# 64-wide matmul products in column pairs, one merged weight in the first message round, and a GpSimd memset behind each gather, in a four-layer graph kernel

## The chip, the cores and the metric

The kernel runs on one NeuronCore of one Trainium2 chip. The metric is device time in microseconds (us). Three runs of the kernel before gave 3177.02, 3179.41 and 3182.76 us; the median is 3179.41 us. A profile comes from one further execution, recorded by the hardware profiler.

Engines are named as the profile names them: PE (TensorE matmul), PEld (its weight loads), DVE (VectorE), ACT (ScalarE), POOL (GpSimd), SP (SyncE, which issues DMAs).

## The reference

There are B = 16 graphs of N = 1024 nodes with C = 64 channels, a dense weighted adjacency of 1024 x 1024 for each (about 1.6% of it non-zero), H = 128 hidden channels, and four layers, each of which adds its result to `x` and normalises over channels:

```
x = layernorm(x + (adj @ (x @ W0) + b0))                 # layer 0
adj_d = dilate(adj)            # drops some neighbours by rank
agg = sum over tau of w * quantile_tau(x of the kept neighbours)
x = layernorm(x + (relu((x + agg) @ W1 + b1) @ W2 + b2)) # layer 1
h = x @ W_embed                                           # layer 2
for l in range(3): h = relu(adj @ (h @ Wl[l] + bl[l]))
x = layernorm(x + h @ W_proj + b_proj)
t = adj @ x                                               # layer 3
x = layernorm(x + where(t > 0.5, 1, 0))
```

The quantiles of layer 1 need, for every node and channel, the neighbours' values in order. That is where most of the VectorE work lies.

## The kernel before

Nodes lie in T = 8 tiles of P = 128. Everything is float32 unless it is named otherwise. The work on one graph is cut into generator functions whose `yield` values are estimated times:

- `words_of` (L502) loads eight rows of the adjacency (`arow`, by SP), transposes each on PE (L439), copies it out on ACT (L441), packs its non-zero pattern into words (L526, L536), and runs layer 0 through `Layer0.feed` (L464) and `Layer0.end` (L472 to L490). The transposed rows go to DRAM (`adjd`, L532).
- `front` and `listing` turn the words into a sorted list of neighbour numbers per node (`idx`), sort the nodes by degree, and write the table of `x` rows to DRAM (`table`).
- `gathered` (L808) fetches neighbour rows. Slot k of a tile of 128 nodes is one indirect DMA of 128 rows x 66 floats from the table, issued by GpSimd at L815. The eight tiles form five groups (`GROUPS`, L30). Partly filled slots are packed, so that one graph takes 122 gathers of whole slots and 7 of packed ones. A group's gathers land in a buffer of tag `x`, of which there are four. So the gathers of a group wait until the buffer of the fourth group before it has been summed.
- `masked` (L847) marks the slots that don't count (ACT L868) and makes the quantile weights. `quantiles` (L891) sorts each group's slots by a comparison network on DVE (L906). `summed` (L916) scales the wanted ranks (ACT L932) and adds them on PE (L936).
- `back` (L1122) is the rest of layer 1, and layers 2 and 3. `to_nodes` (L955) brings the aggregate back from degree order to node order by one-hot products in bf16 (L979) and adds x (L985). Two products, `residual` and `layernorm` follow. Then `to_channels` (L362) and the product with `we_sb` (L1185) make the embedding, and each of three message rounds multiplies by `wl_sb` (L1196), copies (L1199), and multiplies by the adjacency (L1207), followed by a relu (L1210). Layer 3 is `aggregate` (L372, product L377), a transpose back (L1219), a comparison and a layernorm.

The order in which the instructions stand on each engine is fixed at build time: a heap at L1266 takes the generator with the smallest due time, lets it record its next step, and puts it back with its yield value added (times a stretch factor). The due times come from `LENGTHS` (L52), whose sum is 192.06 us for a graph, and from constants such as `BACK` and `WORDS`. While graph b sorts its groups, the gathers run one to two groups ahead, `words_of` and `front` run for the next graph, and `back` for the graph before.

Some products have only 64 output channels, so that the stationary operand has 64 columns: L464, L377, L979 and L985. They use columns 0 to 63 of the array, and their results lie in PSUM partitions 0 to 63. The two halves of the 1024 nodes are then made one after the other, each with a PSUM bank and an ACT copy of 64 x 512 of its own. In `Layer0` the upper half of the `ax` tile receives x transposed, so that one product with `w0_sb` (W0 above an identity) makes both the new value and the residual; to transpose two tiles at once, `xt` has an extra tile of zeros in front.

Of the kernel before, what the change touches and what calls it, by code (L numbers as in the profile page):

```python
# [10 lines left out]
F32 = mybir.dt.float32  # L11
# [9 lines left out]
P = 128  # L21
# [132 lines left out]
def kernel(  # L154
# [102 lines left out]
    top = const.tile([P, T, K], F32, name="top")  # L257
    nc.vector.memset(top, 0.0)
    flags = const.tile([1, B + 1], I32, name="flags")
    qw = const.tile([P, Q], F32, name="qw")  # L260
    ntau = const.tile([P, Q], F32, name="ntau")
    for s, (tau, w) in enumerate(zip(TAUS, QWEIGHTS)):
# [11 lines left out]
    def load(name, shape, src):  # L274
        t = const.tile(shape, F32, name=name)
        nc.scalar.dma_start(t, src)
        return t


    w0_sb = const.tile([2 * C, C], F32, name="w0_sb")  # L280
    nc.scalar.dma_start(w0_sb[:C, :], w0)
    nc.vector.tensor_copy(w0_sb[C:, :], ident[C:, C:])
    w1_sb = load("w1_sb", [C, H], w1)
    b1_sb = load("b1_sb", [H, 1], b1.unsqueeze(1))
    w2_sb = load("w2_sb", [H, C], w2)
    we_sb = load("we_sb", [C, H], we)
    wl_sb = load("wl_sb", [H, NL, H], wl.rearrange("l i o -> i l o"))
    wp_sb = load("wp_sb", [H, C], wp)

# [5 lines left out]
        nc.vector.tensor_scalar(m, m, 1.0 / C, None, op0=ALU.mult)  # L295
        nc.vector.tensor_scalar(v, v, m, None, op0=ALU.subtract)

    for v, n in ((w0_sb, 2 * C), (w2_sb, H), (wp_sb, H)):
        centred(v, n)


# [17 lines left out]
    ones16 = const.tile([S, P], BF16, name="ones16")  # L319
    nc.vector.memset(ones16, 1.0)  # L320

    def add_bias(bank, first, n, times):

        nc.tensor.matmul(bank[:, :times * n], ones16,
                         bias16[:, first:first + n].unsqueeze(1).to_broadcast([S, times, n]),
                         start=True, stop=False)
# [1 line left out]

    mask_u8 = const.tile([B * T, P], U8, name="mask_u8")
    nc.scalar.dma_start(mask_u8, nodemask.rearrange("b (t p) -> (b t) p", p=P))  # L330
    mask_f = const.tile([B * T, P], F32, name="mask_f")
    nc.vector.tensor_copy(mask_f, mask_u8)
    mask = const.tile([P, B * T], F32, name="mask")
    pm = ps.tile([P, HALF], F32, tag="mm", name="pm", bufs=2)
# [7 lines left out]
    def psum_mm():  # L342
        return psum("mm", 2)

    def psum_tp():
        return psum("tp", 2)
# [12 lines left out]

    def to_channels(dst, src):  # L362

        for h in range(NH):
            pt = psum_mm()
            for i in range(TH):
                nc.tensor.transpose(pt[:C, i * P:(i + 1) * P], src[:, h * TH + i, :], ident)
            yield 1.5
            nc.scalar.copy(dst[:, h * HALF:(h + 1) * HALF], pt[:C, :])
            yield 1.0  # L370

    def aggregate(dst, adjT, src, bank):  # L372

        for h in range(NH):
            pa = bank()
            for m in range(T):
                nc.tensor.matmul(pa[:C, :], src[:, m, :], adjT[:, h * TH:(h + 1) * TH, m, :],  # L377
                                 start=(m == 0), stop=(m == T - 1))
                yield 1.3
            nc.scalar.copy(dst[:, h * HALF:(h + 1) * HALF], pa[:C, :])  # L380
            yield 0.7

    def layernorm(u, y, who, mean=False):

# [33 lines left out]
        return a  # L418

    def load_x(b):  # L420
        xt = act.tile([P, T + 1, C], F32, tag="x", name="xt")
        nc.vector.memset(xt[:, 0, :], 0.0)
        nc.sync.dma_start(xt[:, 1:, :], one(x, b).rearrange("o (t p) c -> p (o t) c", p=P))
        return xt

    def transposed(b, block, then):
# [25 lines left out]
    class Layer0:  # L452
# [6 lines left out]
        def feed(self, t, at):  # L459
            if t % TH == 0:  # L460
                self.bank = psum_ax()
            cols = slice((t % TH) * P, (t % TH + 1) * P)
            for m in range(T):
                nc.tensor.matmul(self.bank[:C, cols], self.xt[:, m + 1, :], at[:, m, :],  # L464
                                 start=(m == 0), stop=(m == T - 1))
            yield 2.4
            if t % TH == TH - 1:
                h = t // TH
                nc.scalar.copy(self.ax[:C, h * HALF:(h + 1) * HALF], self.bank[:C, :])
                yield 0.7  # L470

        def end(self, y):  # L472
            for h in range(NH):
                pt = psum_tp()
                for i in range(TH):

                    two = self.xt[:, h * TH + i:h * TH + i + 2, :].rearrange("p t c -> p (t c)")
                    nc.tensor.transpose(pt[:, i * P:(i + 1) * P], two, ident)
                yield 1.0
                nc.scalar.copy(self.ax[C:, h * HALF:(h + 1) * HALF], pt[C:, :])  # L480
                yield 0.7
            pz = psum_ax()
            add_bias(pz, 0, C, T)
            for t in range(T):
                nc.tensor.matmul(pz[:, t * C:(t + 1) * C], self.ax[:, t * P:(t + 1) * P], w0_sb,
                                 start=False, stop=(t == T - 1))
                if t % 2:
                    yield 0.7
            yield 1.0
            yield from layernorm(nodes(pz), y, "0")  # L490
# [317 lines left out]
    def gathered(st, g):  # L808
# [5 lines left out]
        def gather(dst, index):  # L814
            nc.gpsimd.indirect_dma_start(  # L815
                out=dst, out_offset=None, in_=st["table"],
                in_offset=bass.IndirectOffsetOnAxis(ap=index, axis=0))

        whole = [(i, t, k) for i, t in enumerate(tiles) for k in range(n)
                 if k < len(ROWS[t]) and ROWS[t][k] == P]  # L820
# [134 lines left out]
    def to_nodes(dst, st):  # L955


        ag = st["ag"]
        pieces = act.tile([P, S, T, C], BF16, tag="msg", name="pieces")
        for i in range(S):  # L960
            nc.scalar.copy(pieces[:, i], ag)
            yield 0.8
            if i + 1 < S:
                nc.vector.tensor_tensor(ag, ag, pieces[:, i], ALU.subtract)
                yield 0.8
        st["moved"] = True
        banks = [psum_mm() for _ in range(NH)]
        for s in range(T):
            ones_at = tmp.tile([P, N], BF16, tag="ones_at", name="ones_at", bufs=2)
            if st["b"] == B - 1 and s % 3:  # L970
                nc.vector.tensor_scalar(ones_at, iota, st["minus"][:, s:s + 1], 0.0,
                                        op0=ALU.add, op1=ALU.is_equal)
            else:
                nc.scalar.activation(ones_at, iota, AF.Abs, bias=st["minus"][:, s:s + 1])  # L974
                nc.scalar.activation(ones_at, ones_at, AF.Relu, bias=1.0, scale=-1.0)  # L975
            yield 1.9
            for h, bank in enumerate(banks):
                for i in range(S):
                    nc.tensor.matmul(bank[:C, :], pieces[:, i, s, :],  # L979
                                     ones_at[:, h * HALF:(h + 1) * HALF],  # L980
                                     start=(s == 0 and i == 0), stop=False)
            yield 1.7
        for h, bank in enumerate(banks):
            for i in range(TH):
                nc.tensor.matmul(bank[:C, i * P:(i + 1) * P], st["x1"][:, h * TH + i, :], ident,  # L985
                                 start=False, stop=(i == TH - 1))
            yield 1.2
            nc.scalar.copy(dst[:, h * HALF:(h + 1) * HALF], bank[:C, :])
        yield 1.0


# [28 lines left out]
    def general(b):  # L1020
# [44 lines left out]
        xc = act.tile([P, T, R], F32, tag="xc", name="xc", bufs=LIVES)  # L1065
        st["x1"] = xc[:, :, :C]
        run(l0.end(st["x1"]))
        xT = act.tile([C, N], F32, tag="chan", name="x1T")
        run(to_channels(xT, st["x1"]))
        xrow = dram.tile([C, N], F32, tag="xrow", name="xrow", bufs=1)  # L1070
        nc.sync.dma_start(xrow, xT)
        st["agg"] = act.tile([P, T, C], F32, tag="x3", name="agg")
        with tc.For_i(0, T, 1) as t:
            nb = tmp.tile([P, N], F16, tag="nb", name="nb")
# [47 lines left out]
    def back(st):  # L1122
# [31 lines left out]
            return act.tile([P, T, C], F32, tag=tag, name=name)  # L1154

        def chan(name):
            return act.tile([C, N], F32, tag="chan", name=name)


        oT = chan("oT")  # L1160
# [8 lines left out]
        for h in range(NH):  # L1169
            cols = slice(h * HALF, (h + 1) * HALF)  # L1170
            ph = psum_mm()
            nc.tensor.matmul(ph, w1_sb, oT[:, cols], start=True, stop=True)
            yield 1.3
            nc.scalar.activation(hT[:, cols], ph, AF.Relu, bias=b1_sb)
            yield 0.7
        x2 = node_tile("x2", "x2")
        yield from residual(hT, w2_sb, C, x1, x2)

        x2T = chan("x2T")
        yield from to_channels(x2T, x2)  # L1180
        hT = act.tile([H, N], F32, tag="hT", name="h0T")
        for h in range(NH):
            cols = slice(h * HALF, (h + 1) * HALF)
            ph = psum_mm()
            nc.tensor.matmul(ph, we_sb, x2T[:, cols], start=True, stop=True)  # L1185
            yield 1.3
            nc.scalar.copy(hT[:, cols], ph)
            yield 0.7
        for l in range(NL):
            msg = act.tile([P, T, H], F32, tag="msg", name="msg")  # L1190
            for h in range(NH):
                pg = psum_mm()
# [20 lines left out]
        yield from residual(hT, wp_sb, 2 * C, x2, x3)  # L1213

        tT = chan("tT")
        yield from aggregate(tT, adjT, x3, psum_mm)
        pt = psum_mm()
        for t in range(T):
            nc.tensor.transpose(pt[:, t * C:(t + 1) * C], tT[:, t * P:(t + 1) * P], ident[:C, :C])  # L1219
        yield 2.0  # L1220
        u = wide_u("u3")
        nc.vector.scalar_tensor_tensor(u, nodes(pt), 0.5, x3, op0=ALU.is_gt, op1=ALU.add)
# [93 lines left out]
```

## Time and profile before

| what | value |
|---|---|
| median of three timed runs | 3179.41 us |
| span of the profiled execution | 4328.2 us |
| PE busy, PE weight loads busy | 2647.8 us, 1635.7 us |
| DVE busy | 2822.0 us |
| ACT busy | 1914.0 us |
| POOL busy | 2160.8 us |
| instructions recorded | 46055 |
| mean granted TensorE clock | 0.764 of full speed |
| DMA | 282.54 MB, mean 65 GB/s |

The profiled execution is known by its span alone: 4328.2 us from the first to the last instruction of the core, 1148.8 us more than the median of the timed runs. "Busy" is the time in which an engine had an instruction under way. Matmul ends are modelled, and spans on POOL are rough, so the distance from one start to the next is the better measure on these two. A matmul of two float32 operands leaves two records; a transpose or a bf16 product leaves one.

### The profile page before, as it was taken

How to read it: one execution, taken by the hardware profiler on the slowest of the kernel's cores; microseconds unless marked ns; L12 is line 12 of the kernel's file. 1: busy time of each engine (PE TensorE's matmuls, PEld its weight loads, DVE VectorE, ACT ScalarE, POOL GpSimd, SP SyncE). 2: the span in 40 equal slices, each digit the busy share in tenths (PEclk: the TensorE clock that was granted, in tenths of full speed). 3: DMA queues.
4: the chain of work that ended last, by engine and by line, in shares of the span. 5: the costliest groups of instructions: out<-in, count | busy, mean ns of one | idle time of the engine just before them, and what ended most of it. 6: DMA issues, size and time to landing. Idle time of an engine off the chain costs nothing.

```text
span 4328.2 us, 46055 instructions
## 1 busy us (share of the span) xinstructions
PE 2647.8 (61%) x13765; PEld 1635.7 (38%) x13766; DVE 2822.0 (65%) x6935; ACT 1914.0 (44%) x6153; POOL 2160.8 (50%) x2078
## 2 busy tenths in 40 slices
PE   6034285675848567584755758476575848456478
PEld 5023152443525244352533435253343525233243
DVE  6058383865849486594857668485766859476671
ACT  2034352634536264453535455363545536253641
POOL 1715626455454645546465464546545554645600
PEclk8566597787969778796877879687787969768688
DMA  3212121322222132222213222231322222111210
GB/s 107 42 50 70 34 67 37 104 54 78 73 71 84 40 101 56 78 77 74 77 39 90 64 83 76 65 84 40 100 60 79 78 80 71 39 57 24 62 43 3
DMA packets 169056, 282.54 MB, mean 65 GB/s; under 512 B 99485, under 2 KB 102112, under 8 KB 166880
## 3 DMA queue, kind: packets, MB, share of 16 engines
q1 hardware_dynamic: 67584, 142.01, 9.9%
q0 software_dynamic: 66048, 69.88, 9.1%
q10 hardware_dynamic: 35168, 67.62, 4.1%
q8 instruction: 114, 1.87, 0.2%
q14 instruction: 142, 1.16, 0.1%
HBM read 204.33 MB, written 71.44 MB: 64 GB/s over the span
## 4 chain that ended last, share of the span: by engine, by line
another core or an unknown queue 28%; DVE 25%; PE 23%; ACT 16%; issue 7%; DMA 0%; ACTq 0%; DVEq 0%
DVE g L906 7%; PE mm L1207 7%; DVE s L906 7%; ACT g L868 6%; ACT ones_at L974 3%; PE ax L464 3%; ACT ones_at L975 2%; PE tp L439 2%; PE mm L377 2%; PE pa L936 2%; PE mm L1196 2%; ACT g L932 1%; PE mm L1141 1%; DVE top L707 1%
## 5 line engine op out<-in xcount | busy, mean ns | idle before, releaser
L815 POOL DMA_INDIRECT g<-table,idx x1952 | 2045.4, 1048 | 1919.7 <-PE pa L936 666.8
L1207 PE MATMUL mm<-adjB,msg 128*128 128x512 f32 x1536 | 769.6, 621 | 109.1 <-issue 82.4
L936 PE MATMUL pa<-g,ident 128*128 128x128 f32 (+1 forms) x1600 | 376.0, 360 | 430.1 <-ACT g L932 300.5
L868 ACT ACTIVATE g<-g,bias 128x64 f32<-128x64 f32 (+9 forms) x2272 | 596.8, 341 | 47.9 <-DVE bias L864 29.2
L906 DVE TENSOR_TENSOR s<-g 128x256 f32<-128x256 f32 (+9 forms) x944 | 531.3, 588 | 64.5 <-ACT g L868 55.5
L936 PEld LDWEIGHTS pa<-g,ident 128*128 128x128 f32 x1600 | 312.3, 248 | 574.0 <-ACT g L932 347.1
L906 DVE TENSOR_TENSOR g<-s 128x256 f32<-128x256 f32 (+8 forms) x864 | 473.4, 573 | 9.0 <-DVE s L906 3.0
L932 ACT ACTIVATE g<-g,w 128x64 f32<-128x64 f32 x1552 | 397.8, 341 | 17.2 <-DVE w L912 13.6
L1207 PEld LDWEIGHTS mm<-adjB,msg 128*128 128x128 f32 x1536 | 268.7, 197 | 301.1 <-issue 270.7
L1147 DVE TENSOR_TENSOR u<-mm,mb 128x512 f32<-128x512 f32 x32 | 22.1, 691 | 463.1 <-remote 313.5
L464 PE MATMUL ax<-at,xt 128*64 128x128 f32 x1920 | 284.5, 310 | 17.4 <-issue 17.4
L377 PE MATMUL mm<-adjB,x 128*64 128x512 f32 x512 | 272.6, 666 | 36.3 <-issue 31.3
L979 PE MATMUL mm<-ones_at,pieces 128*64 128x512 bf16 x768 | 213.0, 420 | 119.0 <-ACT ones_at L975 77.1
L464 PEld LDWEIGHTS ax<-at,xt 128*64 128x64 f32 x1920 | 250.2, 158 | 81.2 <-issue 79.1
L439 PE MATMUL tp<-ident,arow 128*128 128x128 f32 x1024 | 181.7, 309 | 156.2 <-remote 66.4
L399 DVE TENSOR_REDUCE ln_v<-sq 128x8 f32<-128x512 f32 x64 | 43.6, 681 | 296.4 <-issue 156.8
L439 PEld LDWEIGHTS tp<-ident,arow 128*128 128x128 f32 x1024 | 140.9, 162 | 205.1 <-issue 131.7
L441 ACT COPY at<-tp 128x512 f32<-128x512 f32 x240 | 139.0, 580 | 177.2 <-remote 122.3
L906 DVE TENSOR_TENSOR g<-g,s 128x256 f32<-128x256 f32 (+5 forms) x432 | 199.1, 464 | 15.1 <-remote 5.0
L906 DVE TENSOR_TENSOR g<-g 128x256 f32<-128x256 f32 (+8 forms) x304 | 200.7, 660 | 11.2 <-remote 4.0
L1219 PE MATMUL mm<-ident,tT 64*128 64x64 f32 x128 | 25.7, 295 | 293.9 <-ACT tT L380 207.4
L1210 ACT ACTIVATE hlT<-mm 128x512 f32<-128x512 f32 x96 | 57.4, 598 | 296.4 <-PE mm L1207 123.7
(225 smaller groups left out, 4361.9 us busy)
## 6 DMA issues: line engine op xcount, KB each, us to landing
arow<-in_adj_dram SPq DMA_DIRECT2D x128, 512.0 KB
adjd<-at ACTq DMA_DIRECT2D x120, 512.0 KB
adjB<-adjd SPq DMA_DIRECT2D x15, 4096.0 KB
g<-table,idx POOLq DMA_INDIRECT x1952
table<-xc ACTq DMA_DIRECT2D x16, 264.0 KB
xt<-in_x_dram SPq DMA_DIRECT2D x16, 256.0 KB
out_dram<-y SPq DMA_DIRECT2D x16, 256.0 KB
stage<-table,packed POOLq DMA_INDIRECT x112
```

Of the source, the lines that this page charges most:

```text
L377: nc.tensor.matmul(pa[:C, :], src[:, m, :], adjT[:, h * TH:(h + 1) * TH, m, :], start=(m == 0), stop=(m == T - 1))
L439: nc.tensor.transpose(pt[:, i * P:(i + 1) * P], a[:, j * P:(j + 1) * P], ident)
L441: nc.scalar.copy(at[:, h * TH:(h + 1) * TH, :], pt.rearrange("p (i n) -> p i n", n=P))
L464: nc.tensor.matmul(self.bank[:C, cols], self.xt[:, m + 1, :], at[:, m, :], start=(m == 0), stop=(m == T - 1))
L815: nc.gpsimd.indirect_dma_start(out=dst, out_offset=None, in_=st["table"], in_offset=bass.IndirectOffsetOnAxis(ap=index, axis=0))
L868: nc.scalar.activation(v, v, AF.Identity, bias=bias[:m, i, k:k + 1])
L906: nc.vector.tensor_tensor(box(bufs[mode >> 1 & 1], d, run, sd, count), box(bufs[mode >> 3], a, run, sa, count), box(bufs[mode >> 2 & 1], b ...
L932: nc.scalar.activation(slots(g, bufs[0], lo + r, lo + r + 1)[:, i, 0, :C], slots(g, bufs[at[r]], lo + r, lo + r + 1)[:, i, 0, :C], AF.Iden ...
L936: nc.tensor.matmul(pa[:, :(e - k) * nt * C], ident, rows_.rearrange("p (k c) -> p k c", c=R)[:, :, :C], start=(j == 0), stop=(j == len(run ...
L974: nc.scalar.activation(ones_at, iota, AF.Abs, bias=st["minus"][:, s:s + 1])
L979: nc.tensor.matmul(bank[:C, :], pieces[:, i, s, :], ones_at[:, h * HALF:(h + 1) * HALF], start=(s == 0 and i == 0), stop=False)
L1207: nc.tensor.matmul(pg, msg[:, m, :], adjT[:, h * TH:(h + 1) * TH, m, :], start=(m == 0), stop=(m == T - 1))
```

## The change

- **Column pairs.** The products with 64 stationary columns are issued in twos. One of a pair writes PSUM partitions 0 to 63, the other 64 to 127 of the same bank, on columns 0 to 63 and 64 to 127 of the array. In `to_channels`, `aggregate` and `to_nodes` the two are the two halves of the nodes; in `Layer0.feed` they are the even and the odd tiles of the sum, which the next product adds up, since `w0_sb` now holds W0 twice. A channel tile is 128 x 512 instead of 64 x 1024, and one ACT copy takes the place of two. `Layer0.end` adds x by a second product with `self_sb`. Transposes of 64 columns in `to_channels` become products with the identity.
- **Merged weight.** `wel_sb` = W_embed Wl[0] with the bias folded in is made once at the start. The first message round becomes `aggregate` of x + 1 (64 channels), one product with `wel_sb`, and the relu. The embedding product, the first product with `wl_sb` and the first 128-wide product with the adjacency are gone.
- **Memset.** `gather` issues a GpSimd memset of a tile `pause` of 128 x 256 bytes after every indirect DMA.

The constants of the planner are the same; the yield values of the changed steps are smaller or fewer. In the built program PE has 14711 instructions of work instead of 15044 (both with the fallback branch, which was not run), and POOL has one memset after each of its gathers.

```diff
+    pause = const.tile([P, 2 * P], U8, name="pause")
...
+    self_sb = const.tile([2 * C, 2, C], F32, name="self_sb")
+    nc.vector.memset(self_sb, 0.0)
+    w1_sb = const.tile([2 * C, H], F32, name="w1_sb")
+    for h in range(2):
+        half = slice(h * C, (h + 1) * C)
+        nc.scalar.dma_start(w0_sb[half, :], w0)
+        nc.vector.tensor_copy(self_sb[half, h, :], ident[half, half])
+        nc.scalar.dma_start(w1_sb[half, :], w1)
...
+    wel_sb = const.tile([2 * C, H], F32, name="wel_sb")
+    pe = ps.tile([P, HALF], F32, tag="mm", name="pe", bufs=2)
+    for h in range(2):
+        half = slice(h * C, (h + 1) * C)
+        nc.tensor.matmul(pe[half, :H], share16[:, half], bias16[:, 3 * C:3 * C + H],
+                         start=True, stop=False)
+        nc.tensor.matmul(pe[half, :H], weT, wl_sb[:, 0, :], start=False, stop=True)
+    nc.vector.tensor_copy(wel_sb, pe[:, :H])
...
+    def rows_of(t, h):
+        return t[h * C:(h + 1) * C]
...
-    def aggregate(dst, adjT, src, bank):
-        for h in range(NH):
-            pa = bank()
-            for m in range(T):
-                nc.tensor.matmul(pa[:C, :], src[:, m, :], adjT[:, h * TH:(h + 1) * TH, m, :],
+    def aggregate(dst, adjT, src, bank, tiles):
+        pa = bank()
+        for m in range(T):
+            for h in range(NH):
+                nc.tensor.matmul(rows_of(pa, h), src[:, m, :], adjT[:, tiles[h], m, :],
                                  start=(m == 0), stop=(m == T - 1))
-                yield 1.3
-            nc.scalar.copy(dst[:, h * HALF:(h + 1) * HALF], pa[:C, :])
-            yield 0.7
+            yield 1.3
+        nc.scalar.copy(dst, pa)
+        yield 0.7
...
             for m in range(T):
-                nc.tensor.matmul(self.bank[:C, cols], self.xt[:, m + 1, :], at[:, m, :],
-                                 start=(m == 0), stop=(m == T - 1))
-            yield 2.4
+                nc.tensor.matmul(rows_of(self.bank, m % 2)[:, cols], self.xt[:, m, :], at[:, m, :],
+                                 start=(m < 2), stop=(m >= T - 2))
+            yield 1.6
...
+                nc.tensor.matmul(pzt, self.ax[:, t * P:(t + 1) * P], w0_sb, start=False, stop=False)
+                nc.tensor.matmul(pzt, xT[:, t // 2 * P:(t // 2 + 1) * P], self_sb[:, t % 2],
                                  start=False, stop=(t == T - 1))
...
                 in_offset=bass.IndirectOffsetOnAxis(ap=index, axis=0))
+            nc.gpsimd.memset(pause, 0)
...
-            for h, bank in enumerate(banks):
-                for i in range(S):
-                    nc.tensor.matmul(bank[:C, :], pieces[:, i, s, :],
+            for i in range(S):
+                for h in range(NH):
+                    nc.tensor.matmul(rows_of(bank, h), pieces[:, i, s, :],
...
-        x2T = chan("x2T")
-        yield from to_channels(x2T, x2)
+        x2p = act.tile([P, T, C], F32, tag="msg", name="x2p")
+        nc.scalar.activation(x2p, x2, AF.Identity, bias=ones)
+        yield 1.0
+        gT = chan("gT")
+        yield from aggregate(gT, adjT, x2p, psum_mm,
+                             [slice(h * TH, (h + 1) * TH) for h in range(NH)])
...
-                nc.tensor.matmul(ph, we_sb, x2T[:, cols], start=True, stop=True)
+                nc.tensor.matmul(ph, rows_of(wel_sb, h), rows_of(gT, h), start=True, stop=True)
...
-        for l in range(NL):
+        for l in range(1, NL):
```

## Prediction

> **What bounds the kernel now.** I read the profile in the order page, GpSimd's waits, stages, chain of waits. The page first:
>
> ```profile
> span 4328.2 us, 46055 instructions
> PE 2647.8 (61%) x13765; PEld 1635.7 (38%) x13766; DVE 2822.0 (65%) x6935; ACT 1914.0 (44%) x6153; POOL 2160.8 (50%) x2078
> another core or an unknown queue 28%; DVE 25%; PE 23%; ACT 16%; issue 7%; DMA 0%; ACTq 0%; DVEq 0%
> L815 POOL DMA_INDIRECT g<-table,idx x1952 | 2045.4, 1048 | 1919.7 <-PE pa L936 666.8
> L1207 PE MATMUL mm<-adjB,msg 128*128 128x512 f32 x1536 | 769.6, 621 | 109.1 <-issue 82.4
> ```
>
> The span is 1149 us above the median of 3179 us. The chain names the excess: 28% of 4328 is 1212 us of waits for nothing that the program contains. In these stretches PE, ACT and DVE stand still together while POOL goes on gathering. 4328 - 1212 = 3116, near the median, so I take these waits as belonging to the profiled execution and subtract 1149 us from its sums. That is an assumption; no view proves it. The shares of the page then mislead: POOL's 50% is of the wrong span. Its own rows tell more:
>
> ```profile
> 96.05 1.13 POOL L815 DMA_INDIRECT g<-table,idx  x1 [92.94 <-DVE nb L526]
> 97.48 0.95 POOL L815 DMA_INDIRECT g<-table,idx  x1 [0.30 <-issue]
> ...
> 4114.67 1.45 POOL L815 DMA_INDIRECT g<-table,idx  x1 [0.30 <-issue]
> ```
>
> The columns are start, duration, engine. A gather takes 0.95 us when nothing disturbs it, and 0.30 us lie before the next even though it waits for nothing: one per 1.25 us. The waits of POOL give that gap in total:
>
> ```profile
> POOL g L815 <- PE pa L936: 666.8, 42, 80.5
> POOL g L815 <- issue: 566.6, 1858, 0.5
> ```
>
> "issue" is this gap, 1858 times (0.305 us each). The stages before, during and after the gathers:
>
> ```profile
> 0.00:96.00 96.00, 58.83 (x551) 50.72 (x553) 65.84 (x244) 23.23 (x59) 2.45 (x14) 0.84 0.31 94
> 96.00:4115.60 4019.60, 2417.51 (x12660) 1498.03 (x12658) 2672.22 (x6485) 1821.06 (x5889) 2157.84 (x2064) 0.76 0.24 67
> 4115.60:4328.20 212.60, 171.41 (x557) 87.00 (x557) 83.94 (x208) 69.70 (x205) 0.52 (x1) 0.85 0.06 23
> ```
>
> The numbers are the window, its length, and busy PE, PEld, DVE, ACT, POOL. The middle stage, less the excess, is 4019.6 - 1149 = 2871 us for 16 graphs. In it POOL needs 2157.8 busy + 566.6 + 34.7 (gaps before whole and packed gathers) = 2759 us, or 96%; DVE 2672, 93%; PE 2418, 84%. So the tightest engine is the one that the page shows as half idle. POOL has 2871 - 2759 = 112 us left over the whole run, 0.054 us for each of its 2064 gathers.
>
> **Part 1, the memset.** It adds 2064 instructions to POOL, in order behind each gather. Each waits for the memset before it (the same tile), which ended a gather earlier, so the wait is free; but the next gather is queued behind the memset, and `masked` (ACT and DVE) waits for the gathers of its group. No such memset stands in the trace; the nearest are those of the start:
>
> ```profile
> L215 POOL MEMSET tri<- 128x128 f16 x1 | 0.2, 195 | 0.0
> masks.py:197 POOL MEMSET ident<- 128x128 f32 x1 | 0.2, 205 | 0.3 <-POOLq L1302 0.3
> L1302 POOL MEMSET const-float32-0.0<- 128x1 f32 x1 | 0.1, 99 | 0.1
> ```
>
> From 1 to 128 elements the duration rises by 106 ns, 0.83 ns an element; two-byte elements take as long as four-byte ones, so I count elements and not bytes. 256 elements: 0.21 us, and about 0.03 us to start it (the one-element memsets start 0.02 to 0.03 us apart). **Bounds**: below zero I exclude, since no row shows a gather made shorter by an instruction before it; zero, if the memset fits into the 0.30 us gap; 0.085 us, if four bytes are written at once (64 x 0.83 + 30 ns); 0.24 us if it is added whole. Which? The same 0.3 us also stands between the end of PE's last `pa` product and a gather that waited for it (2491.70 to 2491.97), with POOL idle before. So it looks like starting work of the gather itself, after its release, and not like a hole. The Trainium skill, "GPSIMD Engine Reference", Instruction dispatch, speaks both ways: each of the eight cores goes on to the next instruction when its own share is done, and a pair of cores makes the descriptors. By that rule the other six would have the memset for nothing, but the pair, which sets the pace of gathers, pays it whole. By the rule 256 elements at its 1.03 cycles and 1.2 GHz are 0.22 us plus dispatch; by the row 0.24. I take 0.24 us, nearest to the measured memsets: 2064 x 0.24 = **+495 us** on POOL.
>
> **Part 2, the pairs.** A matmul of two float32 operands is two records. One graph has, with spacings from stretches in which they ran close together:
>
> - L464: 128 records; 16 of them filled 1.96 us, with their 16 weight loads 1.72 us. So 15.7 us.
> - L377: 32 records, 16.6 us.
> - L979: 48 records of bf16, 12 in 2.75 us: 11 us.
> - L985: 16 records, as L464: 2 us.
>
> If the two of a pair run together, half goes: 23 us. Here the Trainium skill has a rule against it: "TensorE: Matmul & The Clock Gate", The mechanism, says that a weight load overlaps a running matmul only if the two use different row groups, and column pairs share their rows. The trace shows loads beside matmuls of one tile now, at 1.72 of 1.96 us. By the row L464 can't fall below its loads: 13.8 us instead of 7.9; by the rule, loads and matmuls in turn, a pair would take 4 x 0.107 + 0.246 = 0.67 us, more than today's 0.49, and L464 21.7 us. For 512 columns loads are small (0.15 of 0.52 us), and half is nearly reached. I take -2, -8, -5 and 0: 15 us for a graph. Two products more with `self_sb` (16 records of 0.12 us) cost 2.
>
> **Part 3, the merged weight.** Gone: 32 records of L1207 (13.7 us by the chain of the last graph), 16 of L1196 on `h0T` (2.4), two bias products (0.8), the 8 transposes at L367 (1.2); in their place an aggregate in pairs, 8.3 us. PE saves 10 us. ACT saves about six copies of 0.58 us and pays two: 2 us. Parts 2 and 3 together: -23 us of PE for each graph.
>
> **What it is worth.** PE is at 84%, and behind it stand POOL and DVE, of which these parts save nothing. Only where PE sets the end does all of it count. That is the tail, 212.6 us with 171 of PE:
>
> ```profile
> 4278.10 13.73 PE mm L1207 x32
> 4298.87 16.57 PE mm L377 x32
> ```
>
> There the last graph's `back` loses 8 (L377), 10 (the round), and a few us at L979, and the graph before it some of the same: -30 us. The start (two waves of L464, 7.1 us each) gives 2 to 7; I say 5. The order on POOL and SP is unmoved; SP issues the same transfers. PE and ACT record `back` and `words_of` in fewer, shorter steps, so these stand earlier among the sort's steps: what DVE waits for comes no later.
>
> **Sum.** Start 96 - 5, gathers 2759 + 495, tail 213 - 30: 91 + 3254 + 183 = **3528 us**, with POOL never waiting. I predict 3530. DVE's cover is gone then: each group's `masked` waits for its gathers, and the freed PE time is idle. The likeliest case reaches from 3430 (0.19 us a memset) to 3570 (some waits remain).
>
> **Rivals.**
>
> 1. *The memset is hidden in the 0.30 us gap.* For it: the memset is shorter than the gap. Against it: the gap behaves as start-up of the gather. POOL's floor is then 91 + 2759 + 183 = 3033 us, and DVE's lies close (93%). From 3179 go 35 us at the two ends and about half of POOL's 112 us of waits, since `summed` frees buffers earlier: 3090 us. Range 3040 to 3140.
> 2. *The memset costs 0.085 us.* 2064 x 0.085 = 175; 3033 + 175 = 3208, and the waits that stay make it up to 3280.
> 3. *The excess isn't the profiler's alone.* If gathers at full pace also hold the other engines up in timed runs, a slower pace loosens that. For it: the stretches in which PE, ACT and DVE stand still end a few us after POOL stops (POOL stops at 2479.2, DVE goes on at 2484.2). Against it: the timed runs have no room for more than 3179 - 3116 = 63 us of it. With those gone too, 3020.
> 4. *The pairs don't overlap.* Worth at most the 35 us at the ends: 3560 instead of 3528, inside the first case.
>
> Rival 1 turns into the forecast at one point: where the memset adds more than (112 + 35) / 2064 = 0.07 us to a gather.
>
> **How the numbers follow.** Forecast 0.55; rival 1 0.31; rival 2 0.08 (nearly all of it slower); rival 3 0.06. Rival 4 is within the forecast. A difference of 0.2% (6 us) is about what a measurement of this kernel can tell. Faster: 0.31 + 0.06, less a little of rival 1 that comes out level: 0.35. Same: 0.04. Slower: 0.61. The range runs from 3050, which leaves out rival 3 and a fifth of rival 1, to 3570.
>
> **What will show it.** In the after profile: POOL memsets of about 0.3 us, 2064 times, and starts of undisturbed gathers 1.49 us apart (1.25 would be rival 1, 1.33 rival 2). POOL's waits for `pa` should be nearly gone, and DVE or ACT should wait for gathers. The span may well fall while the time rises, if the excess of the profiled execution depends on how densely POOL gathers; so the span alone decides nothing. Records of paired products with nearly equal starts show overlap. I am wrong if the gap takes the memset in, or if timed gathers are quicker than profiled ones, which no view of one profile can show.

## The result, and the profile after

After takes 3532.88 us (median of four runs, 3529.20 to 3535.21), before 3179.95 us (3177.02 to 3182.76) on the same chip: 1.1107 times as long, 95% interval 1.1091 to 1.1122. The forecast was 3530. Runs that lie more than 1.5% above the fastest of their kernel are left out of the ratios (this matters for the set of e8 alone). On other chips, told at the end of the experiments, a kernel close to after was faster than before, so this ratio doesn't speak for every chip.

The page of after, with the rows that answer to those shown of before:

```profile
span 3532.3 us, 47411 instructions
PE 2262.5 (64%) x13484; PEld 1437.6 (41%) x13485; DVE 2845.3 (81%) x6933; ACT 1855.9 (53%) x6041; POOL 2940.8 (83%) x4142
POOL 70%; PE 9%; DVE 9%; issue 9%; DMA 1%; ACT 1%; POOLq 0%; ACTq 0%; DVEq 0%
L842 POOL DMA_INDIRECT g<-table,idx x1952 | 2119.1, 1086 | 424.7 <-issue 321.5
L845 POOL MEMSET pause<- 128x256 uint8 x2064 | 699.4, 339 | 1.3
```

The span is now the time of a run. Waits for "another core or an unknown queue" are gone from the chain, 70% of which lies on POOL: 50 points are gathers, 17 are memsets. POOL's part of the timeline in a stretch without disturbance:

```profile
1003.42 0.97 POOL L842 DMA_INDIRECT g<-table,idx  x1 [0.17 <-issue]
1004.39 0.33 POOL L845 MEMSET pause<- 128x256 uint8 x1
1004.88 0.95 POOL L842 DMA_INDIRECT g<-table,idx  x1 [0.17 <-issue]
```

Gathers stand 1.46 us apart; before it was 1.25. The memset lasts 0.33 us, and the gap ahead of the gather has shrunk from 0.30 to 0.17: part of the memset lies where nothing was seen before. The waits of POOL hold nothing but this gap, apart from the first gather, and the other engines now wait for gathers (`bias` is made from `hits`, and `hits` from the gathered rows):

```profile
ACT g L896 <- DVE bias L892: 451.5, 75, 17.1
POOL g L842 <- issue: 321.5, 1942, 0.7
DVE hits L890 <- DMA g<-table,idx: 284.8, 46, 16.4
```

So a run is three stretches: the start up to the first gather, the gathers from the first start to the last end, and the tail. Read from the starts and ends of POOL's instructions in the traces (us). "Waits" adds up POOL's idle stretches of over 1 us among the gathers, and "at graphs" is the part of them that falls on the first gather of a graph, which is every 129th. The time is that of the run or, for more, the median; a trace is of one run (that of e6 took 3257.55).

| kernel | start | gathers | tail | waits | at graphs | time |
|---|---|---|---|---|---|---|
| before (e0_before) | 96 | 2929 | 170 | 0 | 0 | 3196.74 |
| after | 105 | 3283 | 145 | 2 | 0 | 3532.88 |
| pairs and merge, no memset (e1) | 103 | 2997 | 146 | 97 | 96 | 3249.60 |
| memset alone (e2) | 97 | 3298 | 171 | 2 | 0 | 3565.35 |
| merge alone (e5) | 103 | 3080 | 170 | 195 | 186 | 3355.08 |
| pairs alone (e6) | 95 | 2996 | 164 | 107 | 81 | 3271.84 |
| as e1, two yields restored (e7) | 104 | 2915 | 147 | 18 | 16 | 3166.05 |

### The profile page after: what moved, and what is told of

Its sections match the earlier page's. It is cut to its first block, busy times and chain, and to the rows that moved or that the text cites. A ratio compares the mean times of both kernels' runs of the same rounds, so it can differ in the third digit from the quotient of the medians.

```text
span 3532.3 us, 47411 instructions
## 1 busy us (share of the span) xinstructions
PE 2262.5 (64%) x13484; PEld 1437.6 (41%) x13485; DVE 2845.3 (81%) x6933; ACT 1855.9 (53%) x6041; POOL 2940.8 (83%) x4142
## 4 chain that ended last, share of the span: by engine, by line
POOL 70%; PE 9%; DVE 9%; issue 9%; DMA 1%; ACT 1%; POOLq 0%; ACTq 0%; DVEq 0%
POOL g L842 50%; POOL pause L845 17%; PE mm L1240 4%; POOL stage L842 3%; DVE g L934 3%; DVE s L934 2%; PE pa L964 1%; DVE top L734 1%; PE tp L465 1%; PE ax L490 1%; DMA g<-table,idx 1%; DVE kw L737 1%; PE mm L404 1%; PE mm L1229 0%; PE ax L512 0%
## 5 line engine op out<-in xcount | busy, mean ns | idle before, releaser
L842 POOL DMA_INDIRECT g<-table,idx x1952 | 2119.1, 1086 | 424.7 <-issue 321.5
L845 POOL MEMSET pause<- 128x256 uint8 x2064 | 699.4, 339 | 1.3
L964 PE MATMUL pa<-g,ident 128*128 128x128 f32 (+1 forms) x1600 | 416.4, 399 | 411.1 <-ACT g L960 410.1
L1240 PE MATMUL mm<-adjB,msg 128*128 128x512 f32 x1024 | 520.3, 635 | 1.5 <-ACT msg L1232 1.5
L960 ACT ACTIVATE g<-g,w 128x64 f32<-128x64 f32 x1552 | 389.8, 336 | 78.8 <-DVE w L940 77.3
L1240 PEld LDWEIGHTS mm<-adjB,msg 128*128 128x128 f32 x1024 | 189.0, 205 | 150.3 <-issue 146.7
L1007 PE MATMUL mm<-ones_at,pieces 128*64 128x512 bf16 x768 | 172.5, 579 | 110.1 <-ACT ones_at L1003 110.0
L914 ACT ACTIVATE hat<-iota,npos 128x10 f32<-128x10 f16 (+2 forms) x384 | 114.1, 297 | 188.7 <-DVE npos L903 188.5
L563 PE MATMUL tp<-pow,nb 128*128 128x65 f16 x1024 | 61.8, 204 | 224.8 <-DVE nb L553 207.5
L678 PE MATMUL wd<-hi,perm 128*128 128x71 f16 x960 | 116.6, 239 | 97.7 <-DVE perm L673 97.7
L678 PEld LDWEIGHTS <-perm 128*128 128x128 f16 x960 | 98.3, 127 | 158.4 <-DVE perm L673 131.1
```

The source lines that it names most:

```text
L678: nc.tensor.matmul(pw[:, :hn], ws, hi[:, t, :], start=False, stop=False)
L842: nc.gpsimd.indirect_dma_start(out=dst, out_offset=None, in_=st["table"], in_offset=bass.IndirectOffsetOnAxis(ap=index, axis=0))
L845: nc.gpsimd.memset(pause, 0)
L914: nc.scalar.activation(h, iota[:, lo:lo + kw], AF.Abs, bias=npos[:, i, s:s + 1])
L960: nc.scalar.activation(slots(g, bufs[0], lo + r, lo + r + 1)[:, i, 0, :C], slots(g, bufs[at[r]], lo + r, lo + r + 1)[:, i, 0, :C], AF.Iden ...
L964: nc.tensor.matmul(pa[:, :(e - k) * nt * C], ident, rows_.rearrange("p (k c) -> p k c", c=R)[:, :, :C], start=(j == 0), stop=(j == len(run ...
```

## The experiments

All ratios are to the kernel before, run on the same chip in the same set; 95% intervals in brackets. The kernels came to run on four chips: e1 to e4 on one (before there: 3173.93 us), e0 and e5 to e7 on a second (3181.10), e8 to e10 on a third (4473.63), e11 on a fourth (4347.26). Each chip was used in one set only, so a property of the chip and one of the hour aren't told apart. The record names neither the chip of the result, where before took what it takes on the first two, nor that of the first profile.

### The parts apart, and the size of the memset

**e2_memset_only**: before, with the memset and nothing else (`mask_f` is moved to make room).

```diff
+    pause = const.tile([P, 2 * P], U8, name="pause")
...
+            nc.gpsimd.memset(pause, 0)
```

> The kernel before with the memset behind each gather and nothing else of the change (one tile of the start moved to make room). Theory: POOL needs 96 + 2064 x 1.59 + a tail of 150 to 213 us: 3530 to 3590 us. Rival (the memset costs only beside the pairs): 3180 us. The span of the profiled execution should lie within 1% of the time.

3565.35 us, 1.1229 [1.1212, 1.1246], as expected. Against before on the same chip that is 391 us, or 0.190 us for each of the 2064 memsets. Against after it lacks only pairs and merge: 32 us (39 by the two ratios to before, as the chips may differ), of which the table puts 26 into the tail.

**e1_no_memset**: after without the memset.

```diff
-    pause = const.tile([P, 2 * P], U8, name="pause")
...
-            nc.gpsimd.memset(pause, 0)
```

> The changed kernel without the memset; pairs and merged weight stay. Theory (the memset lengthens every gather on POOL, and POOL sets the time): the spacing of gathers goes back from 1.59 to about 1.34 us on average, POOL's floor is 105 + 2759 + 183 = 3047 us, and with some waits left the time is 3050 to 3110 us, likeliest 3085. Rival (the time of the pairs or of the merged weight is what was lost): no faster than the kernel before, 3180 us or more. Rival (PE relief is worth only the two ends): 3145 us. In the profiled execution the waits of unknown origin should be back and the span well above the time, if dense gathers bring them.

3249.60 us, 1.0244 [1.0230, 1.0258]: a miss. Pairs and merge save PE work, and without the memset they lengthen the run. The waits of POOL say where:

```profile
POOL g L841 <- issue: 569.3, 1868, 0.3
POOL g L841 <- DVE nb L553: 100.1, 1, 100.1
POOL g L841 <- DMA table<-xc: 62.4, 7, 9.0
```

The first gather of a graph waits for that graph's table (the second row is the start). The last steps of one table, from the timelines of DVE, PE, ACT and POOL, and the write of the table from the chain of waits:

```profile
1389.22 0.29 DVE L596 TENSOR_TENSOR gone<-in_tile,gone 128x128 f16<-128x128 f16 x1
1391.40 1.03 PE L1227 MATMUL mm<-wl_sb,hlT 128*128 128x128 f32 x4
1392.26 1.04 PE L1238 MATMUL mm<-adjB,msg 128*128 128x512 f32 x2
1393.13 0.35 PE L601 MATMUL wd<-gone,back_to 128*128 128x16 f16 x8
1395.10 0.18 ACT L607 COPY xc<-wd 128x16 f32<-128x16 f32 x1
1395.32 5.30 DMA table<-xc
1401.38 0.95 POOL L841 DMA_INDIRECT g<-table,idx  x1 [8.86 <-DMA table<-xc]
```

The operand `gone` is done at 1389.51, but the products that take it (`wd`, L601) stand on PE behind products of `back` (`mm`, L1227 and L1238) and start 3.6 us later. Their copy stands on ACT behind other copies. Then comes the DMA of 5.3 us, and POOL has stood since 1392.5. No cost of a single step is at fault here: the steps stand in another order than before, because the diff lowered the yield values by which the planner orders them (`words_of` from 82.1 to 74.0 for a graph, `back` from 192.4 to 157.7), and left the stretch factors as they were. How late the table is can be read for every graph. In e0 its write is issued 16 to 25 us before the last gather of the graph before ends; in e1, at ten of fifteen boundaries, 3 to 4 us after it.

**e3_memset_1**: after with a memset of one element.

```diff
-            nc.gpsimd.memset(pause, 0)
+            nc.gpsimd.memset(pause[:, :1], 0)
```

> The memset writes 1 byte in each partition instead of 256. Theory (cost of 0.83 ns an element on POOL, plus a start): 255 x 0.83 ns = 0.21 us less for each gather, so the spacing is 1.38 us and POOL's floor 105 + 2848 + 183 = 3136 us; time 3110 to 3170. Rival (any instruction between two gathers costs the whole): 3530 us.

3254.48 us, 1.0261 [1.0245, 1.0276]: outside what was expected, and the same as e1 within their ranges. The timeline of POOL:

```profile
1004.30 0.94 POOL L842 DMA_INDIRECT g<-table,idx  x1 [0.19 <-issue]
1005.24 0.12 POOL L845 MEMSET pause<- 128x1 uint8 x1
1005.55 0.95 POOL L842 DMA_INDIRECT g<-table,idx  x1 [0.19 <-issue]
```

Still 1.25 us from start to start, with an instruction more: the gap shrank from 0.30 to 0.19 us and gave the memset its 0.12. From 1 to 256 elements the memset grows from 0.12 to 0.33 us and the spacing by the same 0.21: 0.8 ns an element, all of it paid. As in e1, POOL waits at the boundaries of two graphs, some 90 us in all, and that is what the forecast of 3110 to 3170 lacked.

**e4_two_memsets**: after with the memset issued twice.

```diff
             nc.gpsimd.memset(pause, 0)
+            nc.gpsimd.memset(pause, 0)
```

> Two memsets of 256 bytes behind each gather instead of one. Theory: the second has no gap to lie in, so it adds its 0.21 us of elements and its start, 0.24 to 0.33 us: 2064 times that is 495 to 680 us, time 4030 to 4210 us. Rival (the time isn't POOL's): far less than 400 us more.

4294.68 us, 1.3541 [1.3520, 1.3561], more than expected: the second costs (4294.68 - 3532.88) / 2064 = 0.369 us, twice the first. Its timeline shows the gap still at 0.15, as after at 0.17, and nothing of the second memset hidden in it:

```profile
1003.79 0.33 POOL L845 MEMSET pause<- 128x256 uint8 x1
1004.18 0.31 POOL L846 MEMSET pause<- 128x256 uint8 x1
1004.64 0.95 POOL L842 DMA_INDIRECT g<-table,idx  x1 [0.15 <-issue]
```

### Before again, and the order of the steps

**e0_before**: before, unchanged, for a second profile.

> The kernel before once more, for a second profile. Theory A (the 1149 us of unnamed waits belong to that one profiled execution): the span is within 1% of the time, 3150 to 3210 us, and gathers take about 1.10 us as in the other profiles, which puts POOL at 2064 x 1.405 = 2900 us of it. Theory B (this program's profiled executions always have them, because its gathers are dense): a span near 4300 us; the changed kernel without the memset has gathers as dense and shows none, which speaks against B.

3196.74 us, in a set in which before took 3181.10. Its page has no excess:

```profile
span 3195.0 us, 46055 instructions
PE 2496.9 (78%) x13765; PEld 1548.3 (48%) x13766; DVE 2824.4 (88%) x6935; ACT 1909.8 (60%) x6153; POOL 2303.1 (72%) x2078
POOL 40%; PE 21%; DVE 16%; issue 13%; ACT 5%; DMA 4%; ACTq 0%; DVEq 0%; POOLq 0%
```

Here POOL never stops: among 2064 gathers no gap is over 0.31 us. A gather takes 1.115 us on average, against 1.046 in the profile that the prediction had, and one comes every 2929 / 2064 = 1.419 us. The length of a gather goes with the work of DVE beside it. Gathers during which DVE stands still take 0.95 us on average in both profiles, those during which it is busy for over nine tenths of the time 1.11 (first profile) and 1.13 us (e0). The first profile has 743 of the former kind, e0 has 40.

**e5_merge_only** and **e6_pairs_only**: one part each, without the memset. In e5:

```diff
-        for l in range(NL):
+        x2p = act.tile([P, T, C], F32, tag="msg", name="x2p")
+        nc.scalar.activation(x2p, x2, AF.Identity, bias=ones)
+        yield 1.0
+        gT = chan("gT")
+        yield from aggregate(gT, adjT, x2p, psum_mm)
...
+        for l in range(1, NL):
```

> The kernel before with the merged weight alone: no pairs, no memset. Theory C (the loss of the version without memset comes from the planner's order, which follows the yield values, and most of these changed with layer 0's pairs): about the time before, 3140 to 3190 us. Theory D (a shorter back is itself what puts the table late): 3220 us or more.

In e6 all paired products stay, and the embedding and three rounds as before:

```diff
-            nc.tensor.matmul(ph, rows_of(wel_sb, h), rows_of(gT, h), start=True, stop=True)
+            nc.tensor.matmul(ph, rows_of(we_sb, h), rows_of(x2T, h), start=True, stop=True)
...
-        for l in range(1, NL):
+        for l in range(NL):
```

> The changed kernel without the memset and without the merged weight: the first round as before, its channel tile in pairs. Theory C: as slow as with the merged weight, 3220 to 3270 us. Theory D: near the time before, 3140 to 3190 us.

e5: 3355.08 us, 1.0553 [1.0537, 1.0570]. e6: 3271.84 us, 1.0299 [1.0283, 1.0315]. Theory C failed for e5, where D's 3220 or more came; e6 came 2 us above C's range. Either part alone is slower, against its own before, than both together. In e5 POOL waits at most boundaries of two graphs, for the table or for what comes just ahead of it:

```profile
POOL g L830 <- DMA table<-xc: 119.8, 8, 17.7
POOL g L830 <- DVE nb L542: 100.4, 2, 100.1
POOL g L830 <- DVE s L921: 57.8, 5, 15.8
```

Together with the column "at graphs" this says where the time goes: e5 lost 174 us and waits 186 at boundaries, e6 lost 91 and waits 81. From the fourth boundary to the last but one e5 issues its table 8 to 13 us, e6 up to 4.5 us after the last gather of the graph before.

The two also part the start: the first gather begins at 103.2 us with the merge's set-up (making `wel_sb`) and at 95.1 with the pairs'.

**e7_words_yields**: as e1, with the yields of `words_of` near their sum before.

```diff
-            yield 1.6
+            yield 2.4
...
-            yield 0.7
+            yield 2.4
```

> Pairs and merged weight without the memset, and the yield values of layer 0 set so that words_of has the length that it had before (82.1 instead of 74.0). The instructions are the same, only their order on the engines moves. Theory C: the 9 us for which POOL waits for the table at each graph go, and with them about 75 us: 3140 to 3190 us. Rival (pairs or products cost the time themselves, or the back's shorter yields do): 3230 us or more.

3166.05 us, 0.9954 [0.9941, 0.9968]: 84 us less than e1 (whose before took 7 us less) by two numbers that only the planner reads. Its table is issued 1 to 25 us before the last gather of the graph before ends. The waits of 9 us are gone, and in the view only the first table is left:

```profile
POOL g L841 <- issue: 569.3, 1868, 0.3
POOL g L841 <- DMA table<-xc: 101.3, 1, 101.3
POOL stage L841 <- issue: 31.1, 102, 0.3
```

At six boundaries that lead is only 1 to 3 us, less than the DMA takes, and waits of 2 to 4 us are left there (16 us in all, which the view puts down to DVE and PE). e1's loss was one of order. For e5 that isn't shown: its `words_of` is unchanged, only `back` is shorter (192.4 to 180.8), and the merge's own chain of steps is a rival that no run rules out.

### Other chips

Two runs were to settle the share of `back`'s stretch, and a third the cost of the memset on top of e7.

**e8_words_back**: e7, with the factor of `back`. **e9_merge_back**: e5, likewise.

```diff
-WORDS_STEPS, LISTS_STEPS, BACK_STEPS = 82.0, 74.0, 181.0
+WORDS_STEPS, LISTS_STEPS, BACK_STEPS = 82.0, 74.0, 148.4
```

In e9 the number is 170.1.

> Pairs and merge without the memset, as e7, and the stretch of back restored as well (BACK_STEPS 181.0 to 148.4, the ratio 157.7 / 192.4 of its sums of steps). Order theory: the 18 us of table waits that e7 still has shrink further and nothing else gates GpSimd, so 3140 to 3170 us, with e7's 3166 as the upper end. Rival (back's order is without weight, words_of alone feeds the table): same as e7 within 0.3%. Second rival (a later back makes its sharers of PE and of the bank late): 3180 to 3260, with new waits of GpSimd for PE pa or for the table.

> The merge alone, as e5, with the stretch of back restored (BACK_STEPS 181.0 to 170.1, the ratio 180.8 / 192.4 of its sums of steps). Order theory: e5 was slow only because back's shorter sum moved its steps against those of words_of; the waits of 15 to 17 us at the graph boundaries go, 3170 to 3230 us. Work theory: the merge's own work (a wait inside the longer chain x2p, gT, h0T, or the buffer msg that x2p takes) holds the engines ahead of the table; the waits stay and the time is 3320 to 3380 us.

**e10_words_memset**: e7 with the memset of after.

```diff
+            nc.gpsimd.memset(pause, 0)
```

> e7 with the memset of 256 elements behind each gather. Pace theory: GpSimd needs 0.17 us more per gather whatever the order of the steps; 2064 x 0.17 = 351 on e7's 3166 makes 3517, and the memset's idle cover takes e7's 18 us of waits in: 3495 to 3535 us, the same as after within 1%. Rival (after owes part of its time to the moved order as the kernels without a memset do): nearer to 3450, 2.3% under after.

On this chip before took 4473.63 us (43 runs, 4420.69 to 4529.01), e8 4549.17 (4475.24 to 4586.26), 1.0101 [1.0066, 1.0136], and e9 4479.09, 1.0018 [0.9991, 1.0046]. e10 took **3517.89 us, 0.7871** [0.7826, 0.7916]. The first lines of the chain of waits, of e9 and of e10:

```profile
DVE 39%; another core or an unknown queue 24%; PE 14%; ACT 12%; issue 9%; POOL 1%; DMA 1%; DVEq 0%; ACTq 0%; SPq 0%
```

```profile
POOL 74%; issue 10%; DVE 7%; PE 7%; ACT 1%; DMA 1%; POOLq 0%; another core or an unknown queue 0%; ACTq 0%; DVEq 0%
```

e9 shows the picture of the first profile of before: waits for nothing that the program contains. So that excess doesn't belong to one execution under the profiler: on this chip all three kernels without a memset (before, e8, e9) pay it in timed runs. The timeline of e9 shows what a burst of gathers does to PE:

```profile
1001.72 0.94 POOL L830 DMA_INDIRECT g<-table,idx  x1 [0.30 <-issue]
1001.85 0.22 PE L644 MATMUL wd<-eq,allones 128*128 128x68 f16 x1 [1.71 <-issue]
1002.55 0.10 PEld L647 LDWEIGHTS <-allones 128*128 128x128 f16 x1 [2.00 <-issue]
1002.96 0.94 POOL L830 DMA_INDIRECT g<-table,idx  x1 [0.30 <-issue]
1003.25 0.38 PE L647 MATMUL wd<-below,allones 128*128 128x272 f16 x1 [1.19 <-issue]
1003.96 0.10 PEld L644 LDWEIGHTS <-allones 128*128 128x128 f16 x1 [1.30 <-issue]
```

Products of 0.2 to 0.4 us and the weight loads between them, with no wait that the profile shows but "issue", start 0.70 us apart or a multiple of it, so that two products stand 1.40 or 2.10 us apart; gathers follow at 1.25 us. The burst began at 974.75, and up to 994 us PE still started its instructions close together; in other bursts this lasted up to some 50 us. The last gather of this burst ends at 1017.6 us; a late ACT step that had stood for 33.55 us starts at 1022.87, and DVE at 1023.50. A burst ends when the next group's buffer is not yet summed (POOL waits 853 us in all for the products `pa` that sum); then the others recover, and so on. With 1.46 us from gather to gather none of it occurs in e10. From e8, on the same chip, e10 differs by the memset and by the factor of `back` alone.

What each run had to tell: e10's pace theory holds (3495 to 3535 expected). On e8 and e9 nothing is settled, since the stalls cover what the order does.

**e11_words_memset_128**: e10 with 128 elements.

```diff
-    pause = const.tile([P, 2 * P], U8, name="pause")
+    pause = const.tile([P, P], U8, name="pause")
```

> e10 with a memset of 128 elements instead of 256 (0.22 us instead of 0.33, undisturbed gathers about 1.35 us apart). Two cases, told apart by what the kernel before takes beside it. Where before takes about 3180 us: linear theory, half of what 256 elements cost over e7, 3166 + 176 = 3340 us (3290 to 3370); rival, the part under the 0.30 us gap is free and the rest is not, 3166 + 2064 x 0.04 = 3250. Where before takes about 4470 us: pace theory, in bursts at 1.25 us a gather the other engines come to a stand after some 20 us and go on 4 us after the burst, so about 4 us of 34 gathers are in arrears, which puts the pace that can be held at about 1.37 us: at 1.35 the arrears grow 6 times more slowly than at 1.25 and a burst of 34 ends before they bite, 3300 to 3450 us. Rival, only a pace of 1.46 holds: 4300 us or more.

4088.97 us, 0.9417 [0.9345, 0.9490], on a chip where before took 4347.26: between the pace theory's 3300 to 3450 and its rival's 4300 or more, so neither was right. Its memset:

```profile
L845 POOL MEMSET pause<- 128x128 uint8 x2064 | 467.0, 226 | 13.8 <-remote 9.8
```

Gathers stand 1.34 us apart, and many bursts go on for 82 gathers, two for 129 (in e9, after the first graph, POOL stops after at most 48), before the same standstill comes; 18% of the chain is left to unknown waits. An instruction behind the gather is not enough by itself; the pace counts. If the third and fourth chips are alike in this, which wasn't tested, the pace that holds lies between 1.34 and 1.46 us. The 1.37 us that I had worked out from what a burst leaves behind lies in that span but is not shown.

## Why the prediction came out

The bound was right: POOL sets the time, and the memset adds to it. That the sum came out within 0.1% is luck: 91 + 3254 + 183 became 105 + 3283 + 145, and inside the middle term two errors of 170 and 141 us cancelled.

- **The excess.** That 1149 us can be subtracted held for the time: e0, on a chip where before takes what it took for the result, has none of them. "Belonging to the profiled execution" is wrong. On two of four chips timed runs of before carry 1166 and 1293 us more than its 3181. The first profile may have been taken on such a chip: its span of 4328.2 and its granted clock of 0.764 are close to before's runs on the fourth (4333 to 4383, clock 0.760 to 0.767). Rival 3, to which I gave 0.06, had the right mechanism for these chips: gathers at full pace hold up the other engines, and a slower pace loosens that. Where before takes 3180 it has nothing to win.
- **POOL as the bound.** Right, and stronger than worked out: the 112 us of slack did not exist, as e0's gathers have no gap over 0.31 us. The step that failed is the 1.337 us a gather. It is 1.419: 170 us too little over 2064. Of these, 143 are the gathers' own length (2158 us in the first profile, 2301 in e0), as DVE stands still beside many gathers in the first profile. The rest are gaps: all 2064 have the 0.305 us, 629 us in all, and I had counted only the 601 that the waits call "issue".
- **The memset.** Taken at 0.24 us, 495 us in all. Measured over the gathers' stretch: 3283 - 2929 = 354 us, 0.17 each, 141 too much (e2 against its own before gives 0.19). The price of an element was right: 0.83 ns from the start's rows, 0.8 measured. The estimate from the Trainium skill's 1.03 cycles an element and 1.2 GHz ("GPSIMD Engine Reference", Elementwise — side-by-side cycle accounting), 0.22 us for 256 elements, agrees with the growth of 0.21. The reading of the gap was half wrong. "Start-up of the gather and not a hole" holds for 0.15 to 0.19 of its 0.30 us, which stay ahead of the gather in every run with a memset; the rest takes in another instruction, as e3 shows with 0.12 us. Summed over the traces, the time between two gathers grew from 0.305 to 0.503 us and the mean gather fell from 1.115 to 1.087, which makes the 0.17. DVE is busy for 0.87 instead of 0.93 of the gathers' time; by the lengths above that explains about 0.01 of the 0.028 us (an estimate), and the rest is open. That the pair of cores making the descriptors pays the memset whole, as the prediction put it, no run shows (the Trainium skill tells of the pair in "When to use GPSIMD" of that page, not in Instruction dispatch).
- **Rival 1** took everything up to 256 elements to be hidden. e3 is its case in fact, with a memset that is hidden; even so it took 3254, and e7, without a memset and nearly without late tables, 3166 instead of 3090. Its base was the same 1.337.
- **The pairs.** The weighing of row against rule went wrong at L464. By the Trainium skill ("TensorE: Matmul & The Clock Gate", The mechanism) a load passes under a running product only where the row groups differ (the section excepts loads into a background weight buffer, which I left out); by my row the loads remained as a floor. Groups of before (L464) and after (L490), products first:

```profile
L464 PE MATMUL ax<-at,xt 128*64 128x128 f32 x1920 | 284.5, 310 | 17.4 <-issue 17.4
L464 PEld LDWEIGHTS ax<-at,xt 128*64 128x64 f32 x1920 | 250.2, 158 | 81.2 <-issue 79.1
```

```profile
L490 PE MATMUL ax<-at,xt 128*64 128x128 f32 x1920 | 158.0, 317 | 0.0
L490 PEld LDWEIGHTS ax<-at,xt 128*64 128x64 f32 x1920 | 127.7, 160 | 63.4 <-issue 62.8
```

  As many records of nearly the same mean length in half the busy time: loads of a pair overlap each other too. A stretch in which they run close together shows it at first hand:

```profile
1030.23 1.04 PE L490 MATMUL ax<-at,xt 128*64 128x128 f32 x16
1030.24 0.80 PEld L490 LDWEIGHTS ax<-at,xt 128*64 128x64 f32 x14 [0.29 <-issue]
```

  16 records take 1.04 us instead of 1.96, which is below the floor of 1.72 that I set; the records of a pair start 3 to 4 ns apart. By the busy sums that is 7.9 us a graph instead of 2 (6.0 against e0's 254.6 us). L377 gave the 8 predicted (272.6 to 144.9 us over 16 graphs; 6.2 against e0's 244.4), L979 2.5 instead of 5 (213.0 to 172.5); it waits 110 us for `ones_at` from ACT. The eight products with `self_sb` took 4.8 us of PE a graph (77.3 us over 16) instead of 2.
- **PE in all.** -23 us a graph was forecast; against e0 it is 234 / 16 = 15, at different granted clocks (0.875 before, 0.727 after), so the work itself fell by more than the busy time shows (a record of L377's product lasts 611 ns in e0 and 663 after).
- **The ends.** The tail gave 26 of 30 us, but from 170 (e0) and not 213, which was again the first profile's regime. The start was to lose 5 and gained 9: I left out the merge's set-up, which e5 and e6 place there (103.2 against 95.1). Both parts together are worth 32 to 39 us beside the memset (e2), 35 forecast.
- **"What DVE waits for comes no later."** Wrong, and hidden in the result only because POOL, slowed by the memset, comes later than the table, which after issues 26 to 32 us before the last gather of the graph before ends. Without it (e1) parts 2 and 3 cost 76 us over the 3173.93 of before on that chip, through the planner's order.

Open: what it is in the third and fourth chips that makes bursts stall; why the table comes later still when the merge stands alone (5.5%); what after itself does there, since only e10 (after with two yields changed) was run. e10 is within 0.5% of after's time though the two stand on different chips.

Of what was run, e7 is the fastest where before takes 3180 (0.9954, a gain of 0.5%) and e10 where it takes 4470 (0.7871). Neither was run on the other kind of chip.

## What to carry to other kernels

If one profile holds a thousand microseconds that the timed runs lack, don't subtract them and read on: its durations are those of another regime, and the regime may be another chip's everyday one; take a second profile, and time on more than one chip. When an edit makes steps shorter in a kernel ordered by estimates, the order moves with the estimates: keep the old numbers first, and change them by a test of their own. To price an instruction on the bounding engine, measure it at two sizes and doubled: what of it lies in a gap is free, once.

## What the runs showed of the hardware that was not expected

- On two of four chips, indirect DMAs of GpSimd in dense succession (1.25 us apart) bring PE, ACT and DVE nearly to a stand after some 20 to 50 us; in e9 PE then starts its instructions only every 0.70 us or a multiple. At 1.46 us it doesn't occur (e10), at 1.34 us later and less (e11).
- An instruction of 0.12 us between two gathers is free; one of 0.33 us costs 0.21 in an undisturbed stretch (0.17 to 0.19 over the run), a second one of 0.31 us 0.34 to 0.37.
- An indirect DMA of 128 rows takes GpSimd 0.95 us while VectorE stands still and 1.09 to 1.13 us on average beside a busy one.
- Weight loads of two products on different column halves run at the same time: 1920 of them in 127.7 us instead of 250.2.
